# Hybrid convolution and attention, eight images on one core: the next image's convolution, normalisation and the token mean put in other places

## The chip, the cores and the metric

One core of a Trainium2 chip runs the whole program. The metric is the device time of one execution in microseconds; a time is given as the median of runs. The profile is of one execution on the same core.

The engines by their names in the profile: PE is the matrix engine (PEld its weight loads), DVE the vector engine, ACT the engine for activation functions, POOL the general engine, and SP the engine whose queue issues nearly all DMAs here. All arithmetic is in fp32. PE works off one fp32 matmul as two instructions, so the counts of PE instructions in the profile are twice the counts in the program; transposes are one instruction.

## The reference, cut to what matters

There are 8 images of 32 x 32 positions with 256 channels, `S = 1024` positions ("tokens") each.

```python
# first layer: group norm (32 groups of 8 channels), then convolution beside attention
g = _gn(x)
conv_out = conv3x3(g, conv_w) + conv_b                 # 256 -> 192 channels
k, q, v = split(g @ qkv_w + qkv_b)                     # 8 heads of 8
logits = q @ k.T + rel_w(q) + rel_h(q)                 # relative logits by column and by row
attn = softmax(logits) @ v @ attn_w + attn_b           # 64 channels
x = x + concat([conv_out, attn])
# second layer: tokens
t = x.reshape(8, 1024, 256)
n = layernorm(t)
t = t + softmax(n @ W_q @ (n @ W_k).T / sqrt(128)) @ (n @ W_v) @ W_o + b_o + n
n2 = layernorm(t)
r = softmax(mean(n2, axis=tokens) @ Wr + br)           # one routing per image, two of 8 experts
t = t + layernorm_affine(experts(n2, r) + n2)
```

The mean of `n2` over the tokens of an image is needed only for the routing, after all eight images have passed the attention of the second layer.

## The kernel before, in words

**Phases.** A first phase runs over the images one after the other and does the first layer and the attention of the second; the finished tokens go to DRAM (`Td`). A second phase loads them again and runs the router and the experts. The change is in the first phase.

**Order.** PE's instructions run in the order in which the program is written (`manual_schedule` for PE). The other engines' instructions are ordered by the framework's scheduler, each engine's queue then running strictly in its order. Work is put between other work by generators: a function yields after a few instructions, and another one calls `next` where it wants them.

**One image, in the order of PE:**

1. `conv_layer_attention` (L559). Eight heads are handled in two groups of four and two halves of the queries, which makes four `Unit`s. A unit loads an operand `F` by 24 DMAs on SP: eight pairs of `rh` and `kq` (L436, L440), which the scores read, and eight `rwd` (L447), which the weights read too. In 8 steps a unit computes 16 score tiles (`score`, L464, tile `lg`, two buffers); DVE takes a maximum of each (L472), and after four heads two small operations (L476, L479). `fold` (L481) turns the maxima into a row of `F`: DVE writes `mb` (L490) and three DMAs on SP bring it in (L494). Then `weigh` computes the scores again, with everything added (L504, tile `st`), ACT takes the exponential (L512), and `gather` multiplies by the values (L520, tile `po`). Maxima run `lead` = 10 steps ahead of exponentials. In those ten steps there is nothing to weigh, and the convolution is put there: `conv_steps` (L403) does 8 tiles of 18 matmuls (L411), DVE adds each finished tile to the image (L419). Two tiles are computed ahead of the first score and eleven matmuls go into each step.
2. The last steps have no scores left, only weights and values. There `norm_steps` (L232) of the next image is put: transposes (`tpx`, L243), copies and statistics on DVE (L245, L246), two small matmuls (`pm`, `pv`), a square root on ACT, then the normalised image into `gpad` (L270), shifted copies of it (L284, L285) and copies by tiles `xn` (L278) on Pool, and the bias added to the image on Pool (L250).
3. The projection of the heads (`pp`, L623).
4. `attention_layer` (L627): layer norm, transposes (`tpn`, L647), keys, queries (`pq`, L662), values, scores (`lg1`), softmax, products (`po1`, L730) and projection (`pa1`, L742). Its `fill(us)` calls put in `input_steps` (L289) of the next image: keys and queries (`pk`, L296), values (`pvv`, L329), the relative logits by column (L364, "w") and by row (L367, "h", tile `prel`), and transposes of the first (`tpw`, L396).
5. The token mean: once the deviations of the second layer norm are known (`rs2`, L772 to L774), 16 matmuls of one column each (L781), two instructions each, and one for the correction (L788), into `pmt`; then `Td` is stored.

The loop over images begins with the load of the next image into `T`, which has two buffers, so that the load reuses the buffer of the image before:

```python
for b in range(B):
    T[b + 1] = load_image(b + 1) if b + 1 < B else None
    ...
    conv_layer_attention(b, ..., norm_steps(b + 1, nxt) ...)
    ...
    attention_layer(b, fill)
    fill(1000.0)
```

The tile pools of PSUM are `lg` (2 buffers of two banks), `st` (3) and `po` (1).

Of the kernel before, what the change touches and what calls it, by code (L numbers as in the profile page):

```python
# [16 lines left out]
P = 128  # L17
# [18 lines left out]
def kernel(  # L36
# [54 lines left out]
    with ExitStack() as ph:  # L91
# [17 lines left out]
        def lg_tile(name):  # L109
            return ps_lg.tile([P, 2, 512], FP, tag="lg", name=name)  # L110

# [120 lines left out]
        def norm_steps(b, held):  # L232


            both = f_tile("x").rearrange("p a e s -> p a (e s)")
            xT = both[:, 0].rearrange("p (k s) -> p k s", k=KC)
            st = work.tile([P, KC, 2, 6], FP, tag="gst", name="gst", bufs=2)
            mv = work.tile([P, KC, 2], FP, tag="gmv", name="gmv", bufs=2)
            for kc in range(KC):
                for q in range(2):  # L240
                    tp = st_tile("tpx").rearrange("p (j t) -> p j t", j=4)
                    for j in range(4):
                        nc.tensor.transpose(tp[:, j, :], T[b][:, q * 4 + j, kc * P : (kc + 1) * P], ident)  # L243
                    dst = xT[:, kc, q * 512 : (q + 1) * 512]
                    nc.vector.tensor_copy(dst, tp.rearrange("p j t -> p (j t)"))  # L245
                    nc.vector.bn_stats(st[:, kc, q, :], dst)  # L246
                    yield
                nc.vector.bn_aggr(mv[:, kc, :], st[:, kc].rearrange("p q s -> p (q s)"))
# [12 lines left out]
            yield  # L261
# [5 lines left out]
            nc.vector.reciprocal(gr, gr)  # L267
            for kc in range(KC):
                xv = xT[:, kc, :].rearrange("p (h w) -> p h w", w=WW)
                nc.vector.tensor_scalar(  # L270
                    gpad[:, 1, kc, 1 : HH + 1, :], xv, gm[:, kc, :], gr[:, kc : kc + 1], ALU.subtract, ALU.mult
                )

            xn = both[:, 1].rearrange("p (k j t) -> p k j t", k=KC, j=NT)
# [7 lines left out]
            for kc in range(KC):  # L282
                mid = gpad[:, 1, kc, 1 : HH + 1]
                nc.gpsimd.tensor_copy(gpad[:, 0, kc, 1 : HH + 1, 1:WW], mid[:, :, 0 : WW - 1])  # L284
                nc.gpsimd.tensor_copy(gpad[:, 2, kc, 1 : HH + 1, 0 : WW - 1], mid[:, :, 1:WW])  # L285
            held["xn"] = xn
            yield

        def input_steps(b, held):  # L289


            kq = work.tile([P, S], FP, tag="kq", name="kq")
            for q in range(2):
                pk = st_tile("pk")
                for kc in range(KC):
# [7 lines left out]
                    yield 0.86  # L303
# [23 lines left out]
            for j in range(NT):  # L327
# [8 lines left out]
                yield 0.43  # L336
# [17 lines left out]
            for which in range(2):  # L354
                for half in range(2):
                    prs = lg_tile("prel")
                    for i in range(16):
# [16 lines left out]
                        if i % 4 == 3 and i < 15:  # L374
                            yield 0.7
# [13 lines left out]
                    yield 0.7  # L389

            for t2 in range(NT // 2):
# [9 lines left out]
                yield 0.43  # L401

        def conv_steps(b):  # L403

            n = 9 * KC
            for t in range(NT):
                pc = st_tile("pc")
# [14 lines left out]
        class Unit:  # L422
# [91 lines left out]
            def gather(self, j, parts):  # L514

                if self.po is None:
                    self.po = ps_po.tile([P, 512], FP, tag="po", name="po")
# [41 lines left out]
        def conv_layer_attention(b, kq, rh, rwd, rwq, ahead):  # L559
# [5 lines left out]
            conv = conv_steps(b)  # L565
            left = NT * 9 * KC - 2 * 9 * KC
            lead = NT + LAG
            for _ in range(2 * 9 * KC):
                next(conv)
            for s in range(NU * NT + lead + 2):  # L570
# [21 lines left out]
                else:  # L592
                    if weigh:
                        units[w].weigh(k, (1, 3), lg_tile)
                        units[w].weigh(k, (0,), st_tile)
                        units[w].weigh(k, (2,), st_tile)
                    if gather:
# [3 lines left out]
                if not weigh and left:  # L601
                    todo = -(-left // (lead - s))
                    for _ in range(todo):
                        next(conv)
                    left -= todo
                if s % NT == 0 and 0 < u <= NU:
                    units[u - 1].fold(u - 1)
                if s > NU * NT:
                    next(ahead, None)
            for _ in ahead:  # L610
                pass
# [13 lines left out]


        def attention_layer(b, fill):  # L627


# [23 lines left out]
            fill(5.6)  # L653

# [71 lines left out]
            def gather(ib):  # L726
                po = ps_po.tile([P, 512], FP, tag="po", name="po1")
# [49 lines left out]
            fill(2.0)  # L777
            pmt = st_tile("pmt")
            for kc in range(KC):
                for t in range(NT):  # L780
                    nc.tensor.matmul(  # L781
                        pmt[:, kc : kc + 1],
                        lhsT=T[b][:, t, kc * P : (kc + 1) * P],
                        rhs=m[:, t, 1:2],
                        start=t == 0,
                        stop=t == NT - 1,
                    )
# [4 lines left out]
            nc.sync.dma_start(out=Td[b], in_=T[b])  # L792

        with tc.manual_schedule(engines={mybir.EngineType.PE}):
            held = {}
            for _ in norm_steps(0, held):
                pass
            for _ in input_steps(0, held):
                pass
            for b in range(B):  # L800
                T[b + 1] = load_image(b + 1) if b + 1 < B else None
                nxt = {}
                conv_layer_attention(
                    b,
                    *(held[k] for k in ("kq", "rh", "rwd", "rwq")),
                    norm_steps(b + 1, nxt) if b + 1 < B else iter(()),
                )
                steps = input_steps(b + 1, nxt) if b + 1 < B else iter(())

                def fill(us):  # L810
                    while us > 0:
                        took = next(steps, None)
                        if took is None:
                            break
                        us -= took

                attention_layer(b, fill)
                fill(1000.0)
                held = nxt
                del T[b]  # L820

# [266 lines left out]
```

## Time and profile before

| | us |
|---|---|
| time, median of 3 runs (lowest to highest) | 2812.09 (2807.95 to 2813.89) |
| the profiled execution's own time | 2810.18 |
| its span, first to last instruction | 2808.4 |
| PE busy | 2676.2 |
| DVE busy | 1358.4 |
| ACT busy | 972.9 |
| Pool busy | 292.4 |
| granted PE clock, mean over the span (1 is full) | 0.935 |

One image in the profile, the fourth, by its stages (times from the start of the span; the other images lie within a few microseconds):

| stage | from | to | us | mean granted clock |
|---|---|---|---|---|
| end of the last projection (`pa1`) to the first exponential's matmul (L504) | 896.2 | 969.1 | 72.9 | 0.91 |
| scores and weights together | 969.1 | 1048.5 | 79.4 | 1.00 |
| end of the first layer, with the next image's norm | 1048.5 | 1087.3 | 38.8 | 1.00 |
| `pk` to `pq`: next image's inputs beside the layer norm | 1087.3 | 1121.8 | 34.5 | 0.63 |
| attention of the second layer | 1121.8 | 1175.5 | 53.7 | 0.98 |

A row of a timeline gives the start, the time, the engine, the line and the instructions. The granted clock is the share of PE's full clock that the chip's throttle let through. SP's rows are the issuing of DMAs, not the transfers.

### The profile page before, as it was taken

Reading aid. Unit: us, or ns where it says so; the run is one execution under the profiler, and the core shown is the slowest. Engines: PE = TensorE matmul, PEld = TensorE weight load, DVE = VectorE, ACT = ScalarE, POOL = GpSimd, SP = SyncE. Lnnn points to the kernel's source line nnn. Section 1 sums busy time; section 2 is a strip of 40 time slices with the busy share of each in tenths; the row PEclk is TensorE's granted clock in tenths of the full one; section 3 lists DMA queues with packets and bytes.
Section 4 is the critical chain, followed back from the end, with each engine's and each line's share of the span. In section 5 each row is a group of like instructions: output and inputs, shape, how many; then the busy total and the mean of one; then the engine's idle time right before and its main releaser. Section 6 shows DMA issues by size and latency. Waiting matters only on the chain.

```text
span 2808.4 us, 42236 instructions
## 1 busy us (share of the span) xinstructions
PE 2676.2 (95%) x17737; PEld 1643.9 (59%) x17737; DVE 1358.4 (48%) x2415; ACT 972.9 (35%) x1614; POOL 292.4 (10%) x319
## 2 busy tenths in 40 slices
PE   5999999999999999999999999999999879999998
PEld 4735673567357735773576367636763456666665
DVE  3574357335733573367336733673366343322332
ACT  0054305431543164316431542163226422222222
POOL 5003000300030003000300030003000121111110
PEclk7998899889988998999799989997999979999999
DMA  3510141014102410242023202320322031121110
GB/s 96 86 33 20 38 85 33 21 49 73 33 21 54 68 33 21 56 66 34 20 59 63 34 20 62 61 34 20 66 41 34 1 109 60 60 75 60 60 53 23
DMA packets 83757, 135.86 MB, mean 48 GB/s; under 512 B 12000, under 2 KB 40552, under 8 KB 81520
## 3 DMA queue, kind: packets, MB, share of 16 engines
q1 hardware_dynamic: 80976, 131.20, 21.0%
q8 instruction: 140, 2.29, 0.4%
q10 hardware_dynamic: 2592, 1.97, 0.2%
q14 instruction: 49, 0.40, 0.1%
HBM read 53.43 MB, written 25.17 MB: 28 GB/s over the span
## 4 chain that ended last, share of the span: by engine, by line
PE 90%; DVE 4%; ACT 3%; DMA 2%; issue 1%; POOL 0%; ACTq 0%; SPq 0%; DVEq 0%
PE pc L411 14%; PE lg L464 14%; PE po L520 9%; PE py L1019 8%; PE phd L1001 8%; PE st L504 8%; PE po L730 4%; PE prel L364 3%; PE lg L699 3%; PE pq L662 2%; PE prel L367 2%; PE tp L719 2%; PE pmt L781 2%; PE py L1016 1%; ACT PT L512 1%; PE tpn L647 1%
## 5 line engine op out<-in xcount | busy, mean ns | idle before, releaser
L512 ACT ACTIVATE PT<-st 128x512 f32<-128x512 f32 (+1 forms) x944 | 541.6, 633 | 863.0 <-PE st L504 862.9
L472 DVE TENSOR_REDUCE my<-lg 128x32 f32<-128x1024 f32 x512 | 616.8, 1223 | 256.9 <-PE st L504 129.6
L504 PE MATMUL st<-F,km 32*128 32x512 f32 x2048 | 573.0, 646 | 14.1 <-ACT PT L512 8.1
L464 PE MATMUL lg<-km,F 24*128 24x512 f32 x2048 | 484.0, 636 | 0.0
L411 PEld LDWEIGHTS pc<-convw,gpad 128*128 128x128 f32 x2304 | 387.3, 196 | 60.7 <-issue 59.9
L411 PE MATMUL pc<-convw,gpad 128*128 128x192 f32 x2304 | 412.6, 338 | 0.0
L520 PE MATMUL po<-PT,v 128*32 128x256 f32 (+1 forms) x3200 | 310.6, 456 | 2.9 <-ACT PT L512 2.7
L520 PEld LDWEIGHTS po<-PT,v 128*32 128x32 f32 x3200 | 64.2, 108 | 315.2 <-issue 282.4
L504 PEld LDWEIGHTS st<-F,km 32*128 32x128 f32 x2048 | 194.2, 185 | 85.5 <-ACT PT L512 44.4
L1019 PE MATMUL py<-w,hT 128*128 128x256 f32 x1024 | 237.3, 385 | 0.0
L464 PEld LDWEIGHTS lg<-km,F 24*128 24x128 f32 x2048 | 135.9, 183 | 152.1 <-issue 107.0
L1001 PE MATMUL phd<-n2T,w 128*128 128x512 f32 x512 | 224.2, 596 | 0.0
L1019 PEld LDWEIGHTS py<-w,hT 128*128 128x128 f32 x1024 | 190.1, 190 | 45.4 <-issue 22.4
L250 POOL TENSOR_TENSOR T<-T,l0b 128x2048 f32<-128x2048 f32 x8 | 36.2, 4524 | 1562.3 <-PE tpx L243 1562.3
L1026 DVE TENSOR_TENSOR r<-py,n 128x256 f32<-128x256 f32 x64 | 27.2, 425 | 310.8 <-PE py L1019 310.8
L1001 PEld LDWEIGHTS phd<-n2T,w 128*128 128x128 f32 x512 | 97.3, 192 | 115.2 <-issue 108.0
L730 PE MATMUL po<-pt,qkv 128*128 128x256 f32 x512 | 116.6, 381 | 11.3 <-DVE pt L722 11.3
L1008 ACT ACTIVATE hT<-phd,b1c 128x512 f32<-128x512 f32 x128 | 86.3, 686 | 96.9 <-PE phd L1001 96.7
L699 PE MATMUL lg<-qkv 128*128 128x512 f32 x256 | 119.1, 593 | 0.0
L730 PEld LDWEIGHTS po<-pt,qkv 128*128 128x128 f32 x512 | 96.7, 190 | 36.2 <-DVE pt L722 13.2
L708 DVE TENSOR_REDUCE nm<-lg 128x1 f32<-128x1024 f32 x64 | 78.0, 1219 | 72.5 <-PE lg L699 72.5
L364 PEld LDWEIGHTS prel<-kq,bdw 32*128 32x128 f32 x1024 | 101.5, 291 | 15.5 <-issue 15.0
(213 smaller groups left out, 2482.7 us busy)
## 6 DMA issues: line engine op xcount, KB each, us to landing
F<-rh SPq DMA_DIRECT2D x256, 128.0 KB
F<-kq SPq DMA_DIRECT2D x256, 64.0 KB
F<-rwd SPq DMA_DIRECT2D x256, 64.0 KB
w<-in_L_ffn_W_dram SPq DMA_DIRECT2D x32, 512.0 KB
T<-in_x_dram SPq DMA_DIRECT2D x8, 1024.0 KB
rwd<-rw SPq DMA_DIRECT2D x16, 512.0 KB
Td<-T SPq DMA_DIRECT2D x8, 1024.0 KB
T<-Td SPq DMA_DIRECT2D x8, 1024.0 KB
```

Of the source, the lines that this page charges most:

```text
L364: nc.tensor.matmul(dst, lhsT=lhsT, rhs=kqv[rows, :, a], start=True, stop=True)
L411: nc.tensor.matmul(pc[:, 0:CO], lhsT=gflat[:, dx, kc, t * P + dy * WW : (t + 1) * P + dy * WW], rhs=convw[:, i, :], start=i == 0, stop=i = ...
L464: nc.tensor.matmul(lg[:, a, :], lhsT=self.F[r : r + 24, a, 0, i * P : (i + 1) * P], rhs=KM[self.g][r : r + 24, a].rearrange("p e k -> p (e ...
L472: nc.vector.tensor_reduce(my[:, :, hl], lg.rearrange("p a (y x) -> p y a x", y=WW), AX.XY, ALU.max)
L504: nc.tensor.matmul(st[:, i, :] if len(heads) > 1 else st, lhsT=KM[self.g][r : r + 32, a, e, :], rhs=self.F[r : r + 32, a, e, :], start=Tru ...
L512: nc.scalar.activation(self.pts[j][:, hs, :], st, AF.Exp)
L520: nc.tensor.matmul(self.po[32 * hl : 32 * hl + 32, cols], lhsT=v32[:, j, self.g * HG + hl, :], rhs=self.pts[j][:, hl, cols], start=j == 0, ...
L699: nc.tensor.matmul(lg[:, h, :], lhsT=qk[0][:, i * P : (i + 1) * P], rhs=qk[1][:, h * 512 : (h + 1) * 512], start=True, stop=True,)
L730: nc.tensor.matmul(po[:, 0:IB], lhsT=v1[:, jc, :], rhs=pt[:, jc, :], start=jc == 0, stop=jc == NT - 1)
L1001: nc.tensor.matmul(phd, lhsT=ws[k][0][:, kc, f * P : (f + 1) * P], rhs=n2T[:, kc, q * 512 : (q + 1) * 512], start=kc == 0, stop=kc == KC - 1,)
L1008: nc.scalar.activation(hT[:, k * NF + f, :], phd, AF.Gelu, bias=b1c[:, f, k * B + b : k * B + b + 1])
L1019: nc.tensor.matmul(py, lhsT=hT[:, k * NF + f, j * P : (j + 1) * P], rhs=ws[k][1][:, f, :], start=False, stop=k == TOPK - 1 and f == NF - 1,)
```

## The change

It moves four things.

- **Norm of the next image.** `norm_steps(b + 1)` now runs in the ten steps of the first maxima of image `b` instead of in the last steps: one piece after each step from the third on. The part that writes `gpad` waits until the convolution of image `b` is done. Its transposed image lies in a `pt` buffer, and the copies by tiles are a function of their own, called after the first layer.
- **Convolution.** A class `Conv` holds an image's convolution. After each sixteenth of the relative logits of the next image, four matmuls of that image's convolution follow, 64 in all, into the one `po` tile; `whole()` completes the tile that is begun (72 of 144). The rest runs in the next call of `conv_layer_attention`: 30 matmuls ahead of the first score instead of 36, what is left over the ten steps. The first image has no such work ahead of it and keeps its whole convolution there.
- **Token mean.** Pool multiplies the eight tiles of the finished image by the deviations and adds them up (DVE does it for the last image). `token_mean` then needs three matmuls, which come in the third step of the next image's maxima.
- **Order of the weights in the last steps.** The heads 0 and 2 come ahead of the pair 1 and 3.

```diff
+        def po_tile(name):
+            return ps_po.tile([P, 512], FP, tag="po", name=name)
...
-        def norm_steps(b, held):
-            both = f_tile("x").rearrange("p a e s -> p a (e s)")
-            xT = both[:, 0].rearrange("p (k s) -> p k s", k=KC)
+        def norm_steps(b):
+            xT = pt_tile("xT").rearrange("p (k s) -> p k s", k=KC)
...
             nc.vector.reciprocal(gr, gr)
+            yield None
             for kc in range(KC):
...
+        def by_tiles():
+            xn = f_tile("x").rearrange("p a e s -> p (a e s)")[:, 0 : KC * S]
...
         def input_steps(b, held):
...
                         if i % 4 == 3 and i < 15:
-                            yield 0.7
+                            yield 0.7, True
...
-        def conv_steps(b):
+        def conv_steps(b, place):
             for t in range(NT):
-                pc = st_tile("pc")
+                pc = place[0]("pc")
...
-            conv = conv_steps(b)
-            left = NT * 9 * KC - 2 * 9 * KC
-            for _ in range(2 * 9 * KC):
-                next(conv)
+            left = conv.left
+            go = True
+            first = min(left, 30)
+            conv.run(first)
+            left -= first
...
                     if weigh:
-                        units[w].weigh(k, (1, 3), lg_tile)
                         units[w].weigh(k, (0,), st_tile)
                         units[w].weigh(k, (2,), st_tile)
+                        units[w].weigh(k, (1, 3), lg_tile)
...
-                if not weigh and left:
+                if not weigh:
                     todo = -(-left // (lead - s))
-                    for _ in range(todo):
-                        next(conv)
+                    conv.run(todo)
                     left -= todo
+                    if s > 1 and go:
+                        go = next(between, None)
+                elif s == lead:
+                    for _ in between:
+                        pass
...
-                if s > NU * NT:
-                    next(ahead, None)
...
             fill(5.6)
+            whole()
...
-            fill(2.0)
-            pmt = st_tile("pmt")
-            for kc in range(KC):
-                for t in range(NT):
-                    nc.tensor.matmul(pmt[:, kc : kc + 1], lhsT=T[b][:, t, ...], rhs=m[:, t, 1:2], ...)
+            acc = work.tile([P, C], FP, tag="n", name="acc", bufs=2)
+            if b + 1 < B:
+                part = work.tile([P, C], FP, tag="n", name="part", bufs=2)
+                for t in range(NT):
+                    to = part if t else acc
+                    nc.gpsimd.tensor_scalar(to, T[b][:, t, :], m[:, t, 1:2], None, ALU.mult)
+                    if t:
+                        nc.gpsimd.tensor_tensor(acc, acc, part, ALU.add)
+            else:
...
+            nc.sync.dma_start(out=Td[b], in_=T[b])
+            return acc, mr
+        def token_mean(b, acc, mr):
+            for kc in range(KC):
+                nc.tensor.matmul(pmt[:, kc : kc + 1], lhsT=acc[:, kc * P : (kc + 1) * P], rhs=ones[:, 0:1], ...)
+            nc.tensor.matmul(pmt[:, KC : KC + NT], lhsT=ones, rhs=mr, start=True, stop=True)
...
+            conv = Conv(0)
             for b in range(B):
...
+                conv.place[0] = st_tile
+                conv_layer_attention(b, ..., conv, between())
+                held, conv = {}, Conv(b + 1)
...
                 def fill(us):
                     while us > 0:
-                        took = next(steps, None)
+                        took, small = next(steps, (None, None))
                         if took is None:
                             break
                         us -= took
+                        if small:
+                            conv.run(4)
```

## The prediction

> **What bounds the kernel now.** I read the page's busy times first, then the timeline of one image, the tensor engine's granted clock by stage, and SP's queue. All times are of the fourth image, the others agree.
>
> ```profile
> PE 2676.2 (95%) x17737; PEld 1643.9 (59%) x17737; DVE 1358.4 (48%) x2415; ACT 972.9 (35%) x1614; POOL 292.4 (10%) x319
> PEclk7998899889988998999799989997999979999999
> ```
>
> PE is busy 95% of the span, so only work that leaves PE, PE's idle places or its clock can pay. The clock row dips once or twice an image. The stretches show where (columns: length, busy us of PE, PEld, DVE, ACT, POOL, granted clock, DMA):
>
> ```profile
> 1091.00:1094.50 3.50, 3.50 (x35) 3.43 (x33) 2.38 (x11) 2.47 (x4) 0.00 (x0) 1.00 0.03 6
> 1106.00:1113.00 7.00, 7.00 (x54) 5.86 (x52) 1.11 (x3) 0.06 (x1) 4.86 (x3) 0.50 0.00 0
> 1113.00:1120.00 7.00, 7.00 (x257) 6.92 (x256) 1.30 (x2) 2.53 (x4) 1.11 (x1) 0.50 0.39 154
> 1178.10:1185.30 7.20, 7.17 (x35) 7.20 (x36) 0.09 (x1) 0.95 (x1) 0.00 (x0) 0.52 0.30 100
> 1185.30:1189.00 3.70, 3.70 (x13) 3.70 (x14) 0.39 (x2) 0.00 (x0) 0.00 (x0) 0.55 0.78 229
> ```
>
> In the relative logits (rows two and three) PE is busy throughout but at half clock: they stream only 32 columns per instruction. The value matmuls before them (64 columns) keep 1.00. The token mean (row four, one column each) is cold too, and the first convolution after it starts cold. The chain of waits over the image's end:
>
> ```profile
> 1174.37 1.15 PE pa L742 x4
> ...
> 1177.78 0.21 DVE mv L774
> 1177.99 0.14 issue
> 1178.13 6.72 PE pmt L781 x32
> 1184.85 0.43 PE pmt L788 x2
> 1185.29 13.51 PE pc L411 x72
> 1198.80 1.07 PE lg L464 x8
> ```
>
> PE waits 2.6 us for the deviations, spends 7.2 us on the mean, then convolves. Last, SP's queue in the next lead (start, time, what):
>
> ```profile
> 905.77 0.39 SPq L104 DMA_DIRECT2D T<-in_x_dram  x1
> 906.21 0.62 SPq L436 DMA_DIRECT2D F<-rh  x1
> ...
> 948.10 4.84 SPq L447 DMA_DIRECT2D F<-rwd  x8
> 965.44 30.90 SPq L494 DMA_DIRECT2D F<-mb  x6
> ```
>
> From the image load to the last of the F loads SP issues for 47.2 us (44.8 to 52.0 over six images, middle 47.3), and only then the F<-mb that the first exponentials need. Now there are 12.5 us to spare.
>
> Let zero be the end of an image's last projection matmul (1175.5 in the chain, 896.2 in the SP rows). The first exponential's matmul (L504) starts at +71.5 in five of the six following leads, +72.9 in one.
>
> **Term 1, convolution between the relative logits (seven images): +17.4 us each.** Now the stretch from pk (L296) to pq (L662) takes 33.4 to 34.9, mean 34.2. The change adds 72 convolution matmuls (144 instructions): sixteen blocks of four, and eight at the end. An instruction takes 162.5 ns at full clock, the first of a block 100 ns more. A block: 1.4 us and 0.2 for switching in and out. Does the clock stay up? From the records I computed, per 3.41 us (the step in which the granted clock changes), the array's use: columns streamed times the share of rows and columns used, over what the full clock could do. The clock fell after use of 0.34 or less, held from about 0.4, and rose from 0.5 only after 0.39 or more. A mixed step is about 0.55 (four convolutions, 3072 column-passes, in 2.2 to 2.9 us): it holds if entered warm, and pk and pvv before it are warm. Cold it would be 0.32 and stay cold, a rival below. Warm: pk and pvv 7.3; eight w steps of 0.92 (pairs every 112 ns, as at 1094.5) plus 1.6: 20.2; eight pairs of LN transposes at 0.34: 2.7; eight h steps of 0.55 (half of 6.98/8, plus 0.1) plus 1.6: 17.2; two waits for the single po tile inside a block, 0.6 each (0.35 for L419 and the handover): 1.2; transposes of rw 1.1; last eight convolutions 2.7. That is 52.4. pq then starts warm: 6.9 instead of about 7.7. Sum +18.2 - 0.8 = +17.4, bounds 15 to 20; times seven, +122. The trace has no h step at full clock; at today's rate the term is 3 us an image higher, inside the bounds.
>
> A page speaks here. The Trainium skill (TensorE: Matmul & The Clock Gate, Part 1) has the clock full after one busy window of about 3.4 us. By busy time that fails: 7.00 busy of 7.00 at clock 0.50. If the page's rule held literally, the logits would gain nothing from company and the total would be some 46 us worse.
>
> **Term 2, norm out of the end of layer one (seven images): -5.1 us each.** From the last lg to the end of pp it takes 38.5 to 40.8 (mean 39.4); in the eighth image, which has no next norm, 34.3. The difference holds four transpose groups, two small matmuls and the Sqrt/Exp table loads. The new order of the heads may give ACT another 0.1 us a step; ACT rests 0.26 to 0.58 there. Sum -36, bounds -30 to -45.
>
> **Term 3, end of image to the first exponential (images two to seven).** Removed: the 2.6 wait, 7.2 of mean, about 1.5 of cold convolution, and half the convolution. What is late next?
> - PE: 30 convolutions 10.0, then ten steps of 1.1 (lg) and 1.6 (four convolutions and a switch), norm 3.3: ends at 40.
> - DVE: from +10.6, eighteen maxima of 1.23 before mb, 22.1; four L476/L479 pairs 2.7; evacuations 0.7; norm copies and statistics 5.5; the small norm steps 2.9 (L258 took 1.6); mcol and mb 1.0; mean 0.4; gaps 1. Ends near +47. The four tpx steps make it DVE's lead, not PE's.
> - SP: the load of the next image reuses the buffer of the finished one and so now waits for Pool's sum instead of PE's mean. In the changed program's order for SP that wait stands, as now, ahead of F's last rh and kq for the first unit, its eight rwd, all of the next two units, and F<-mb. Pool starts at +2.6 and the load needs fifteen operations less the last add: eight multiplies and six adds, 128x256. Nearest rows: L648, 740 ns for such an add; L966, 2852 ns for a 1024-column multiply, 0.75 us for 256 by its slope. I take 0.75 and 0.05 between: 11.2, so the load issues at +13.8 (bounds 0.57, the slope of L250, to 0.9: +11 to +16). Now it issues at +9.6 or so. Then 47.3 of issues, and 2.2 for F<-mb to land (between 2.0 at 1054.5 and 3.3 at 2167.0): +63.3.
>
> The fourth maximum needs the last rh and kq, which landed 8.3 us after the load issue (914.0 against 905.8): PE stands from about +13 to +22, DVE with it, so DVE's end moves to +55. SP's +63.3 still comes last. PE is then idle some 5 us just ahead of the main stage, and may enter it cold: there the use at half clock is near 0.39, so it can last some windows. I take 3 us, bounds 0 to 10. Gain 71.6 - 63.3 - 3 = 5.3; times six, -32.
>
> The other page is on Pool: the Trainium skill (GPSIMD Engine Reference, Engine selection) calls two-input elementwise work about twice as slow there as on VectorE. Rows: 740 ns against 425 for L1026 of that size. Doubling 425 as an estimate, the load would issue at +15.2 and the total be 8 us worse.
>
> **Term 4, image eight:** no load follows and SP is not held. Its F loads ended at +47.7, so +49.9, and 3 for a cold start: -18.6. **Term 5, image one:** the whole convolution stays in its lead, which is PE's: the next norm's transposes add +3. **Term 6, the last mean:** eight DVE operations of 0.48 and three matmuls take the place of 16 cold ones: 0. Td's store keeps its place; Pool's bias and copies for the norm end long before pvv reads them.
>
> Sum: 122 - 36 - 32 - 19 + 3 = +38 us on the profiled execution's own 2810.2 (span 2808.4): 2848. The median of the runs is 1.9 above that: **2850**.
>
> **Rivals.** *The queue keeps up (faster).* Place: SP's stretch between load and F<-mb. Part of its 0.78 us per issue is waiting for landings (the waits put about 17 us an image on F's own loads). If those waits shrink, or Pool's sum is short, DVE's +49 (+47 and landing) sets the lead: -22.5 an image, image eight -31, no restart: 122 - 36 - 135 - 31 + 3 = -77, 2735. It decides as soon as the first exponential comes before about +57 with the clock kept warm 3 us of restart included. Half way is 2790. For it: so much of the wait is landing; against it: the issues alone cost 0.60 and 0.68. *The clock stays half in the mixed stretch.* Each convolution block doubles (+1.3), w steps and transposes stay as now: about +31 an image, 3065. For it: cold use 0.32 is self-keeping; against it: warm entry. Dips at single images would add 31 each. *No change:* the gains just cover term 1, which needs 6 us more per lead.
>
> **How the numbers follow.** About 0.2% (5.6 us) is what a measurement can tell from no change. Main case, slower through terms 1 and 3: 0.66, its own range 2795 to 2925 (term 1 at 15 or 20, load at +11 or +16, restart 0 to 10). Clock half: 0.07. Faster: 0.22. Same: 0.05. The range reaches down to 2765, into the faster case, and leaves out its far end and the cold case.
>
> **What would show it.** The granted clock near 1.00 through the prel lines, and pk to pq near 52; T<-in_x_dram about 14 us after the last pa, waiting for POOL; lg of the second step waiting for DMA F<-kq or F<-rh; L504's first start at about +63 right after F<-mb. Wrong if pk to pq is 45 or less, if L504 starts before +57, or if PEclk falls to 0.5 there.

## The result and the profile after

The changed kernel takes 2935.4 us (median of four runs, 2922.0 to 2937.5) against 2812.5: slower by a factor of 1.043 (95% interval 1.040 to 1.046). The forecast was 2850 with a range of 2765 to 2925: the right sign, and the loss three times as large as forecast. The profiled execution took 2921.98 (span 2919.9), the shortest of its runs, and 111.5 more than the one before by their spans. What follows accounts for these 111.5; the 13 us by which the median lies above the profiled execution are in no trace.

First the page's busy row and clock row. The work on PE is 20 us less, the span 111 us longer: PE now waits. The clock row dips about as often as before, but in other places.

```profile
PE 2655.7 (91%) x17513; PEld 1571.1 (54%) x17513; DVE 1341.5 (46%) x2423; ACT 979.2 (34%) x1616; POOL 381.9 (13%) x424
PEclk8999989997999798989998999889989879999999
```

Next, stretches of the changed kernel (length, busy us of PE, PEld, DVE, ACT, POOL, granted clock, DMA): the relative logits by column and by row with the convolution between them, and then the start of a main stage (from the first exponential's matmul to the last score).

```profile
844.30:862.60 18.30, 17.85 (x173) 16.11 (x172) 3.89 (x8) 1.94 (x3) 6.43 (x7) 0.98 0.04 9
864.50:880.30 15.80, 15.35 (x309) 13.19 (x311) 1.41 (x3) 2.07 (x4) 0.55 (x1) 1.00 0.17 68
1000.70:1007.00 6.30, 0.00 (x0) 0.00 (x0) 0.00 (x0) 0.00 (x0) 1.65 (x2) 0.61 0.44 55
1007.00:1020.00 13.00, 12.86 (x44) 5.43 (x44) 4.35 (x5) 4.56 (x8) 0.00 (x0) 0.50 0.01 1
1020.00:1027.00 7.00, 7.00 (x60) 2.03 (x56) 4.10 (x4) 3.64 (x7) 0.00 (x0) 0.82 0.00 0
```

The logits hold the clock now (0.98 and 1.00 where it was 0.50), but for one step of 3.4 us at half clock around their start, which five of the seven images have. In row three no engine but Pool does anything: PE waits for a DMA. Row four is the price: 13 us at half clock with PE busy all the time.

The lead of that image, by the chain of waits (start, us, what). The image before ended at 938.1.

```profile
952.61 0.93 POOL part L792
953.56 0.39 SPq L104
953.99 0.62 SPq L443
954.66 7.15 DMA F<-kq
961.94 2.04 PE lg L471 x2
...
994.38 0.58 DVE mb L497
...
1000.71 6.39 DMA F<-mb
1007.14 2.10 PE st L511 x6
```

The load of the next image (L104) waits for Pool's last sum; the last kq of the first unit stands behind it, and PE waits for that. DVE has written `mb` at 995.0, but F<-mb goes out only at 1000.7. SP's rows say what it did in between:

```profile
994.26 0.68 SPq L447 DMA_DIRECT2D F<-kq  x1
994.98 4.92 SPq L454 DMA_DIRECT2D F<-rwd  x8
1000.71 2.52 SPq L501 DMA_DIRECT2D F<-mb  x3
```

Last, ACT at the end of the first layer (image eight, all images have it), and PE at the same time:

```profile
2291.24 1.28 ACT L540 ACT_TABLE_LOAD   x1
2292.53 0.20 ACT L540 ACTIVATE tab<-PT 128x1 f32<-128x1 f32 x1
2292.75 1.28 ACT L519 ACT_TABLE_LOAD   x1
2294.04 1.02 ACT L519 ACTIVATE PT<-st 128x1024 f32<-128x1024 f32 x1
2296.55 0.58 ACT L544 COPY os<-po 128x512 f32<-128x512 f32 x1 [1.48 <-PE po L527]
2297.15 1.28 ACT L88 ACT_TABLE_LOAD   x1
```

```profile
2295.12 1.38 PE L527 MATMUL po<-PT,v 128*32 128x512 f32 x6 [3.23 <-ACT PT L519]
...
2300.00 3.67 PE L631 MATMUL pp<-aw,aT 64*128 64x64 f32 x16
```

`tab` (L540) is a one-column square root that brings in its table early; it reads head 2. In the old order head 2 came last. In the new order it is finished before the pair 1 and 3, so ACT loads the table of the square root, then that of the exponential again for the last pair, then the other once more. PE waits 3.2 us for the last pair, and `pp` runs cold (3.67 us, 2.00 where it is warm). The same place in the kernel before, where the load stands behind the last exponential:

```profile
2188.93 2.00 ACT L512 ACTIVATE PT<-st 128x1024 f32<-128x1024 f32 x3 [0.26 <-PE st L504]
2190.95 1.28 ACT L533 ACT_TABLE_LOAD   x1
2192.24 0.20 ACT L533 ACTIVATE tab<-PT 128x1 f32<-128x1 f32 x1
```

The change by stages, in us summed over the images, from the two traces (another 1 us lies between them):

| stage | predicted | measured |
|---|---|---|
| `pk` to `pq`, and the first layer norm's attention behind it | +122 | +121 |
| last score to end of `pp`, eight images | -36 | -8 |
| lead of images two to seven | -50 | -30 |
| main stage of images two to seven | +18 | +35 |
| image eight, lead and main stage | -19 | -13 |
| image one | +3 | 0 |
| after the last projection | 0 | +5 |

### The profile page after: what moved, and what is told of

It reads as the page before. It is cut to its first block, busy times and chain, and to the rows that moved or that the text cites. A ratio compares the mean times of both kernels' runs of the same rounds, so it can differ in the third digit from the quotient of the medians.

```text
span 2919.9 us, 41895 instructions
## 1 busy us (share of the span) xinstructions
PE 2655.7 (91%) x17513; PEld 1571.1 (54%) x17513; DVE 1341.5 (46%) x2423; ACT 979.2 (34%) x1616; POOL 381.9 (13%) x424
## 4 chain that ended last, share of the span: by engine, by line
PE 79%; DVE 8%; DMA 6%; ACT 3%; POOL 3%; issue 1%; SPq 1%; ACTq 0%; DVEq 0%
PE lg L471 13%; PE pc L418 10%; PE po L527 9%; PE py L1072 8%; PE phd L1054 8%; PE st L511 7%; PE po L740 4%; PE lg L709 3%; DVE my L479 3%; PE prel L371 2%; DMA F<-mb 2%; PE pq L672 2%; PE tp L729 2%; PE py L1069 1%; PE prel L374 1%; DMA F<-kq 1%
## 5 line engine op out<-in xcount | busy, mean ns | idle before, releaser
L471 PE MATMUL lg<-km,F 24*128 24x512 f32 x2048 | 567.1, 669 | 56.5 <-DMA F<-kq 55.7
L418 PE MATMUL pc<-convw,gpad 128*128 128x192 f32 x2304 | 447.7, 344 | 6.3 <-DVE T L426 6.3
L527 PE MATMUL po<-PT,v 128*32 128x256 f32 (+1 forms) x3200 | 324.3, 466 | 28.9 <-ACT PT L519 25.9
L471 PEld LDWEIGHTS lg<-km,F 24*128 24x128 f32 x2048 | 169.4, 194 | 246.4 <-issue 119.7
L511 PEld LDWEIGHTS st<-F,km 32*128 32x128 f32 x2048 | 182.7, 192 | 159.5 <-issue 61.5
L1079 DVE TENSOR_TENSOR r<-py,n 128x256 f32<-128x256 f32 x64 | 27.2, 424 | 310.9 <-PE py L1072 310.9
L657 POOL TENSOR_TENSOR T<-T,n 128x256 f32<-128x256 f32 x64 | 47.0, 740 | 705.1 <-DVE n L652 705.1
L553 DVE RECIPROCAL rc<-pa 128x16 f32<-128x16 f32 x32 | 8.2, 257 | 231.1 <-PE pa L550 231.1
```

What stands on the lines that cost most here:

```text
L418: nc.tensor.matmul(pc[:, 0:CO], lhsT=gflat[:, dx, kc, t * P + dy * WW : (t + 1) * P + dy * WW], rhs=convw[:, i, :], start=i == 0, stop=i = ...
L471: nc.tensor.matmul(lg[:, a, :], lhsT=self.F[r : r + 24, a, 0, i * P : (i + 1) * P], rhs=KM[self.g][r : r + 24, a].rearrange("p e k -> p (e ...
L511: nc.tensor.matmul(st[:, i, :] if len(heads) > 1 else st, lhsT=KM[self.g][r : r + 32, a, e, :], rhs=self.F[r : r + 32, a, e, :], start=Tru ...
L527: nc.tensor.matmul(self.po[32 * hl : 32 * hl + 32, cols], lhsT=v32[:, j, self.g * HG + hl, :], rhs=self.pts[j][:, hl, cols], start=j == 0, ...
```

## The experiments

Means by stage of all runs, from their traces (lead: end of the last projection to the first exponential's matmul, images two to seven; main: from there to the last score, images two to eight; tail: to the end of `pp`, eight images). Ends are taken at the start of the last instruction, so a lead is 0.4 us longer here than counted from the prediction's zero. The ratio is to the kernel before, timed on the same chip.

| kernel | lead | main | tail | `pk` to `pq` | median us | ratio (95%) |
|---|---|---|---|---|---|---|
| before | 72.1 | 79.4 | 38.8 | 34.3 | 2812.5 | 1 |
| after | 67.2 | 85.2 | 37.7 | 52.6 | 2935.4 | 1.043 (1.040 to 1.046) |
| e1_order | 67.2 | 84.8 | 34.6 | 50.8 | 2884.1 | 1.025 (1.024 to 1.027) |
| e2_mb_act | 60.3 | 81.2 | 38.4 | 53.0 | 2851.2 | 1.013 (1.010 to 1.015) |
| e3_noconv | 74.9 | 79.3 | 38.2 | 36.8 | 2837.5 | 1.009 (1.007 to 1.011) |
| e4_dvesum | 58.7 | 85.1 | 38.1 | 52.6 | 2882.2 | 1.026 (1.022 to 1.029) |
| e5_order_mb | 61.2 | 81.2 | 34.7 | 51.1 | 2816.1 | 1.002 (1.001 to 1.004) |
| e6_three | 52.5 | 81.2 | 34.9 | 51.1 | 2768.0 | 0.984 (0.982 to 0.985) |
| e7_three_noconv | 64.8 | 81.4 | 34.4 | 35.7 | 2748.6 | 0.977 (0.975 to 0.980) |
| e8_warm | 69.0 | 81.4 | 38.3 | 52.6 | 2916.0 | 1.036 (1.033 to 1.039) |
| e9_load_late | 70.4 | 80.0 | 37.7 | 52.4 | 2913.1 | 1.037 (1.035 to 1.039) |
| e10_mb0_noconv | 64.9 | 106.4 | 34.5 | 34.5 | 2945.1 | 1.047 (1.046 to 1.049) |
| e11_mb0_w | 56.4 | 106.4 | 34.4 | 39.8 | 2915.4 | 1.039 (1.036 to 1.042) |
| e12_mb0_two | 56.9 | 106.7 | 34.5 | 50.7 | 2994.8 | 1.062 (1.057 to 1.067) |
| e13_three_w | 55.3 | 82.0 | 34.4 | 40.3 | 2719.5 | 0.967 (0.966 to 0.968) |

My theory was that four separate costs add up: the convolution between the logits, SP's queue in the lead, the cold start that this brings, and the order of the heads. The rivals were that the lead is DVE's anyway, that the transfers and not the queue are late, and that the mixing alone is to blame.

**The order of the heads alone.**

```diff
-                        units[w].weigh(k, (0,), st_tile)
-                        units[w].weigh(k, (2,), st_tile)
                         units[w].weigh(k, (1, 3), lg_tile)
+                        units[w].weigh(k, (0,), st_tile)
+                        units[w].weigh(k, (2,), st_tile)
```

> The changed kernel with one thing put back: the steps of the tail weigh heads (1,3) before 0 and 2, as before. Theory (the table): the Sqrt table pre-load reads head 2, which in the new order is done before the pair (1,3), so ACT loads Sqrt, loads Exp again for the last pair and loads Sqrt once more; PE waits 3.2 us and projects cold. Then the stretch from the last lg to the end of pp falls from 36.5 to 39.0 to about 34.3 in all eight images, 3.5 us each, and the total falls by about 28 us, to some 2907. Rival (the order of the heads has nothing to do with it; the tail is held by gathers and transposes): the stretch stays at 37 to 39 and the total within 5 us of 2935.

The tail is 34.6 in the mean (34.4 in most images), what the prediction had. `pk` to `pq` behind it gains 1.8 as well. The span is 38 us shorter than the changed kernel's, 25 of it in the tail. The median falls by 51 where I had forecast 28: `pk` to `pq` accounts for 13 more, and the rest is the changed kernel's profiled execution being the shortest of its runs. ACT's rows at the end of image eight have one table load, after the last exponential:

```profile
2257.18 2.00 ACT L519 ACTIVATE PT<-st 128x1024 f32<-128x1024 f32 x3 [0.26 <-PE st L511]
2259.20 1.28 ACT L540 ACT_TABLE_LOAD   x1
2260.49 0.20 ACT L540 ACTIVATE tab<-PT 128x1 f32<-128x1 f32 x1
```

**F<-mb on another queue.**

```diff
-                    nc.sync.dma_start(out=F[r, a], in_=mb[c]...)
+                    nc.scalar.dma_start(out=F[r, a], in_=mb[c]...)
```

> The changed kernel with the six F<-mb loads of each fold issued on ACT's queue instead of SP's. Theory (SP's queue ends the lead): DVE has mb at about +57 after the last projection, and the loads now go out then instead of at +58 to +63; with 2 to 6 us to land the first exponential's matmul comes at +60 to +63 instead of +66 to +69, 25 to 35 us off the total, some 2905; the cold start of the main stage stays. Rival A (the transfers themselves are behind the F<-rwd transfers, whichever queue issues them): first matmul within 1.5 us of +66.8, total within 8 us. Rival B (DVE's maxima end the lead): the same as the theory in time of issue, but no gain at all.

The lead is 60.3, at the lower edge of what the theory said; rivals A and B fall. ACT issues within 0.1 us of DVE's `mb`, and the first matmul follows 3.2 us after the issue instead of 6.4:

```profile
989.08 1.76 ACTq L501 DMA_DIRECT2D F<-mb  x3
992.28 1.40 PE L511 MATMUL st<-F,km 32*128 32x512 f32 x6 [0.51 <-DMA F<-mb]
```

The gain is 84 us, far more than forecast, because with a wait of 0.5 us in place of 4.4 to 9.5 the main stage starts warm too: 81.2 instead of 85.2. I had expected the cold start to stay.

**No convolution between the logits.** The lines `if small: conv.run(4)` are taken out.

> The changed kernel with no convolution between the relative logits: all 144 convolution matmuls of an image stand in its lead, the rest of the change stays. Theory (the moved half costs its full time there, and in the lead it fills time in which PE waits for SP's queue): pk to pq falls from 52.4 to 34 (-18.5 for seven images, -129); the lead takes 23 us more of PE work into about 27 us of idle places, so the first exponential comes at +67 to +71; PE enters the main stage with little idle time before it, so the cold start shrinks by 0 to 5 us an image. Total 2935 - 129 + 15 - 20 = about 2800 (2775 to 2830). Rival (what slows the kernel is the lead itself: the norm and Pool's sum): the lead grows by the whole 23 us of the convolution and the total stays at 2935 - 129 + 160, no faster than before the experiment.

`pk` to `pq` falls by 15.8 and not 18.5, the lead grows by 7.7, the main stage is warm. The rival, a lead longer by 23, falls. At 2837.5 the total misses the range by 7 us; the lead is above what I gave it, since the wait for the last kq stays (the waits have "PE lg L471 <- DMA F<-kq" at 46.9 us in 6 times, against 55.7 in the changed kernel), and the convolution cannot fill it, as it stands behind it on PE.

**The sum on DVE for all images.**

```diff
-            if b + 1 < B:
+            if False:
```

> The changed kernel with the token sum on DVE for all images (eight operations of 0.48 us, as in the last image), none of it on Pool. Theory (the image load waits for Pool's sum and all later issues of SP wait behind it): the load issues at about +7.5 instead of +15.5, SP's chain ends 8 us earlier, and DVE's maxima, 3.5 us later by the sum but no longer stalled as long, end the lead: first exponential at +59 to +63 instead of +66.8, 25 to 45 us off the total, some 2900. Rival (what ends the lead is not SP, but DVE): DVE has 3.5 us more to do and the total rises by up to 20 us.

The load goes out at about +8, and SP's wait for it is 15.5 us in all instead of 61.8:

```profile
SPq L104 <- DVE acc L798: 15.5, 6, 2.7
```

The lead is 58.7, slightly better than forecast, and the total 53 us lower where 25 to 45 were forecast. F<-mb still goes out only when SP is through with the F loads and lands about 6 us later, and the main stage is as cold as before. So the load's wait for Pool is worth 8.5 us an image and the queue another cost of its own.

**Repairs together.** The next three have the old order and F<-mb on ACT (e5), the sum on DVE too (e6), and no mixing besides (e7).

> The changed kernel with the old order of the heads in the tail and F<-mb on ACT's queue, both together; the token sum stays on Pool. Theory (the two costs are separate): lead 60.4 as with ACT's queue alone, main stage 81.2, last lg to end of pp 34.4 and pk to pq 50.6 as with the old order alone; with 52.3 for the first layer's attention and 0.2 that is 279.1 an image against 279 before, a total of about 2800 (2790 to 2815). Rival (ACT is late with the loads once its order is changed back, or the gains overlap): 2835 or more.

> As the kernel before in this list, and the token sum on DVE too, so that the image load does not wait for Pool: all three repairs. Theory (with SP out of the way DVE's maxima end the lead, and the fourth maximum no longer stands for the last kq): first exponential at +50 to +56, main stage 79.4 to 81.2, tail 34.4, pk to pq 50.6, first layer 52.3; 267 to 275 an image, a total of 2715 to 2770, faster than the kernel before the change. Rival (DVE, with 3.9 us of sums more, already ends the lead at +60): no faster than with Pool's sum, about 2800 to 2825.

> All three repairs and no convolution between the relative logits. Theory (72 convolution matmuls cost 16 us there and 23 us where PE sets the time; with the repairs the lead is PE's as soon as it holds the whole convolution): pk to pq 34 to 37, lead 66 to 74, main stage 79.4, tail 34.4, first layer 53.5: 268 to 279 an image, a total 0 to 50 us above that of the three repairs alone. Rival (the mixed stretch is dear and the lead would hold all of it for nothing): the total is 20 us or more below that of the three repairs alone.

The costs add up as stages: e5 is about level with the kernel before, a microsecond above its range, and e6 is faster by 1.6%, at the upper end of its range. In e6 the last 20 us of the lead's chain are DVE's, SP is out of it, and PE goes warm into the main stage:

```profile
949.79 2.27 DVE my L479 x2
...
952.56 0.59 DVE mb L497
953.18 3.16 DMA F<-mb
956.38 1.40 PE st L511 x6
```

That the mixing alone is to blame falls with e6, which keeps all of it and is faster than the kernel before; still, taking it out alone (e3) gave the largest gain of a single change, 98 us. For e7 the theory had the sign wrong and the rival was right to within a microsecond: 19 us faster without the mixing than with it, where I had expected 0 to 50 slower and the rival 20 or more the other way. The mixed half costs 15.4 us between the logits (51.1 against 35.7) and saves 12.3 in the lead, because the lead goes from PE's 64.8 to DVE's 52.5 and no further.

**The cold start alone.** 24 matmuls of the convolution's shape stand ahead of the first exponential's matmul (their sums are used by nothing).

> The changed kernel with 24 more matmuls of the convolution's shape (7.8 us at full clock), whose sums nothing uses, just ahead of the first exponential's matmul of images two to eight, where PE waits 9.5 us for F<-mb. Theory (the idle time ahead of the main stage lets the clock fall, and at half clock the stage's own use of the array does not bring it back for four to six windows): the main stage takes 79.4 to 80.5 instead of 84.4 to 86.8, the lead at most 1 us more; some 35 us off the total, about 2900. Rival (the main stage is longer because DVE or ACT still work off the lead's maxima): it stays at 84 to 87, the total at 2935 or above.

In images two to five the main stage is 79.2 to 79.3, and in the stretch of the fourth the clock stays at 1.00 where the changed kernel had 0.50. In images six to eight it is 83.7 to 84.7: there a wait of 0.9, 2.2 and 4.3 us was left behind the added matmuls. The lead is 1.8 longer, and the total misses the forecast of about 2900 by 16 us. So idle time ahead of the stage, and not work left over on DVE or ACT, is what makes it 5 to 7 us longer. How long the idle time must be is open: 0.9 us was enough in image six, 0.5 us was not in e2, and I did not vary it.

**The load behind the first two units on SP.**

```diff
             units = [Unit(n, kq, rh, rwd) for n in range(2)]
+            if b + 1 < B:
+                T[b + 1] = load_image(b + 1)
...
-                if not last:
-                    T[b + 1] = load_image(b + 1)
```

> The changed kernel with one thing moved: the next image's load stands on SP's queue behind the F loads of the first two units instead of ahead of the first unit's last one. Pool still sums, F<-mb is still on SP. Theory (what costs is that SP stands at the load until Pool is done, not the number of its issues): the first unit's last kq goes out some 13 us earlier, the fourth maximum no longer stands for it, and the first exponential comes at +54 to +61 instead of +66.8; 35 to 75 us off the total, 2860 to 2900. Rival (SP's own issues fill the lead, whatever they wait for): first exponential at +64 or later, total within 15 us of 2935. A second way to miss: the load now lands at about +30, so the transposes of the next image wait for it and hold the maxima behind them on PE.

The theory's number missed, by the way of missing that was named last: the load goes out at +29 to +31, and the transposes of the next norm, which stand in PE's order ahead of the maxima, wait for it.

```profile
964.79 1.57 PE L418 MATMUL pc<-convw,gpad 128*128 128x192 f32 x8
985.80 1.11 PE L245 MATMUL tpx<-ident,T 128*128 128x128 f32 x4 [19.44 <-DMA T<-in_x_dram]
```

The lead grows to 70.4, but the stage behind it starts warm (79.2 to 79.3 in six of seven images), since now DVE is late and not SP: PE waits 0.5 us for F<-mb. The total falls by 22 us, a second sight of the cold start alone. It does not tell the wait at the load from the number of issues; e4 does.

It does settle what made F<-mb slow to land. The loads are on SP's queue here too. In images two to seven the last rwd loads lie 12 us ahead of them, and the first matmul follows 3.2 us after the issue, as from ACT's queue in e2; in image eight they stand right behind rwd loads, and it takes 6.4. The fourth image:

```profile
992.16 4.05 SPq L454 DMA_DIRECT2D F<-rwd  x8
1008.25 1.82 SPq L501 DMA_DIRECT2D F<-mb  x3
```

So rival A of e2 has a part in the cost: some 3 us of the lead are the loads just ahead, the rest is the wait for SP. Whether another queue avoids the 3 us when rwd loads are under way no run shows; in e2 none was issued in the 14 us before.

**F<-mb of the first unit alone on ACT.** `nc.scalar` for n = 0, `nc.sync` for the others, with the other repairs; three amounts of mixing.

> All three repairs and no convolution between the relative logits, but F<-mb on ACT's queue for the first unit of an image alone; the other three units' stay on SP, where nothing waits for them. Theory (the main stage took 81.2 instead of 79.4 because ACT waits for mb and issues nine loads between its exponentials): main stage back to 79.4, lead 64 to 65, total about 2734 (2725 to 2742). Rival (the 1.8 us come from the table load of Exp or from the clock at the start of the stage): main stage 81, total 2748 as with all folds on ACT.

> As the one before in this list, with four convolution matmuls after each step of the relative logits for the width (36 of 144, with the four that complete a block), none after those for the height. Theory (DVE ends the lead at +52, PE at +64 with the whole convolution, so half of what was mixed is free in the lead, and the width's steps, which were cold alone, run at full clock in company): lead 52 to 56, pk to pq 41 to 46 with the height's steps cold again; main stage 79.4; 260 to 268 an image, a total of 2690 to 2720. Rival (a convolution matmul between logits costs its full 0.33 us and more): pk to pq 48 or more, total no better than without mixing.

> As the one before in this list, with two convolution matmuls after every step of the relative logits (36 in all) instead of four after half of them. Theory (the array's use decides the clock): two convolutions with 0.92 or 0.55 us of logits are a use of about 0.40 to 0.45 at full clock, just over what held it so far; if it holds, pk to pq is 39 to 42 and the total 2670 to 2700. Rival (the use of the mixed step lies under what holds the clock): the stretch runs at 0.5, each pair of convolutions takes 1.3 us instead of 0.65, pk to pq 45 to 50, total 2720 to 2750.

All three are failures as wholes, by a cause I had not looked for: their main stages take 106 us. The scheduler's order for SP's queue changed with what is on it. With all F<-mb on SP those of the second unit stood ahead of the fourth unit's loads; here they stand behind them, and these wait for an F buffer. SP in e10, where the exponentials of the second unit wait 23.7 us (the last row joins the loads of two folds):

```profile
441.36 5.72 SPq L454 DMA_DIRECT2D F<-rwd  x8
456.36 0.61 SPq L443 DMA_DIRECT2D F<-rh  x1
...
467.41 5.84 SPq L454 DMA_DIRECT2D F<-rwd  x8
474.00 39.62 SPq L501 DMA_DIRECT2D F<-mb  x6
```

The question of e10, why the main stage is 81.2 and not 79.4 with all folds on ACT, has no experiment that isolates it. Its rival (the table load of Exp, or the clock at the start of the stage) falls by e9, whose ACT loads that table there too, and whose main stage starts warm in six images and takes 79.2 to 79.3 with F<-mb on SP. That leaves the issues on ACT, which the trace of e7 shows: ACT issues F<-mb in the midst of the exponentials and rests 2.85 us around it, and the waits of that stage have a second rest of 2.8.

```profile
429.57 1.87 ACTq L501 DMA_DIRECT2D F<-mb  x3
431.49 1.08 ACT L519 ACTIVATE PT<-st 128x512 f32<-128x512 f32 x2 [2.85 <-DMA F<-mb]
```

The stages ahead of the main one still tell about the mixing. With half of it among the column logits (e11) `pk` to `pq` is 39.8, only 5.3 above none. With two matmuls after every step (e12) there are two sorts of image: 37.5 in two of them, below the theory's 39 to 42, and 48 to 61 in the other five, most of them above the rival's 45 to 50. The same stretches of e12, column logits and row logits of a slow and of a fast image:

```profile
281.30:308.90 27.60, 27.60 (x169) 24.23 (x170) 4.83 (x10) 1.94 (x3) 9.71 (x9) 0.52 0.05 9
311.30:330.20 18.90, 18.90 (x285) 15.39 (x284) 1.05 (x2) 1.66 (x4) 0.00 (x0) 0.50 0.14 56
592.10:607.50 15.40, 15.40 (x171) 13.75 (x170) 5.05 (x10) 1.96 (x3) 7.33 (x9) 1.00 0.09 18
608.70:619.30 10.60, 10.60 (x285) 8.71 (x284) 1.21 (x3) 2.56 (x4) 1.89 (x1) 1.00 0.26 102
```

The work is the same and PE is busy for the whole of both; only the clock differs. By the array's use, worked out from the records as in the prediction, the slow image has about 0.2 to 0.33 in the windows of the cold stretch and the fast one about 0.4 to 0.56: two states that each keep themselves. The Trainium skill (TensorE: Matmul & The Clock Gate, Part 1) gives the clock back after one busy window of about 3.4 us. Here it stays away for the 46.5 us of rows one and two, all of it busy time (as are the 2.4 us between them), so busy time alone does not bring it back; the use fits both images.

**Half of the mixing, all folds on ACT.** Four convolution matmuls after each step of the column logits, none after the row logits, and all repairs.

```diff
                         if i % 4 == 3 and i < 15:
-                            yield 0.7, True
+                            yield 0.7, which == 0
...
-                    yield 0.7, True
+                    yield 0.7, which == 0
```

> All three repairs, F<-mb of all units on ACT's queue, and four convolution matmuls after each step of the relative logits for the width only (36 of 144). Theory (mixing costs less than it saves only as long as the lead is PE's): by the stages of the run with the same half mixed but split queues, pk to pq 40 against 35 without mixing and 51 with all of it, lead 56 against 64 and 53; main stage 81.2; tail 34.4; first layer 52.4: 264.2 an image against 269 without mixing and 273 with all, a total of 2710 to 2730, against 2748.6 and 2768. Rival (mixing never pays, a convolution matmul between logits costs what it costs in the lead): 2745 to 2760, between the two.

2719.5 us: 0.967 of the kernel before (0.966 to 0.968), within the forecast range and the best of all. The clock row has no dip from the second slice to the routing (a slice is 68 us; within it the row logits still fall to half clock, for 3 to 7 us an image):

```profile
PE 2563.4 (95%) x17513; PEld 1539.6 (57%) x17513; DVE 1374.9 (51%) x2479; ACT 955.8 (35%) x1600; POOL 294.9 (11%) x319
PEclk8999999999999999999999999999999979999999
```

The rival (mixing never pays) falls: the first 36 matmuls cost 4.6 us between the logits (40.3 against 35.7), as they keep the column logits at full clock, and save 9.5 in the lead (55.3 against 64.8). The second 36 cost another 10.8 and save only 2.8.

## Why the prediction was right and wrong

**Right.** The direction, and the wait that ends the lead. Term 1 was 52.4 for `pk` to `pq`, measured 52.6; with what follows +122 against +121. The clock held in the mixed stretch, as the use of 0.55 said. The stall of the fourth maximum for kq came where forecast, +14.4 to +24 (forecast +13 to +22). SP's queue ended the lead, not DVE: `mb` was ready at +57 (forecast +55) and issued at +58 to +63. The faster rival had the right bound but needed more than it named: with the load out at +8 (e4) SP still issues F<-mb up to 5 us behind `mb`. Only with F<-mb off SP as well does the first exponential come at +52, before the +57 that the rival named; with the old order of the heads too, the kernel is then faster (e6).

**Term 2 failed by a wrong step**, the largest single error: -36 forecast (bounds -30 to -45), -8 measured, 28 of the 73 us missing from the sum. The prediction took the new order of heads for a matter of 0.1 us a step and looked at ACT's rests. What it left out is that `tab` reads head 2 of the last tile, so that the new order puts the table load ahead of the last exponential. In image eight, whose last steps held no norm before either, one load of 1.28 us became three. The trace of before showed the load right behind the last exponential, and the diff showed what moves; following the one reader of `pt[:, 2]` would have found it. e1 confirms it: 34.6 with the old order.

**Term 3 was right in mechanism and wrong in three sizes**, the restart among them (below); together they miss by 37 us, from -32 to +5. The first exponential came at +66.8 in the mean, not +63.3. Pool's pair of operations took 1.83 us a tile (0.92 and 0.72 and gaps), not 1.6: the load went out at +15.5 instead of +13.8. SP's chain behind it was a little shorter than the 47.3 taken. But F<-mb took 5.0 to 6.9 us from issue to use, not 2.2. Eight rwd transfers had been issued just before it; from the same queue, 12 us behind them, it took 3.2 (e9). The two sizes make 20 us over six images. The Trainium skill (GPSIMD Engine Reference, Engine selection) calls two-input elementwise work about twice as slow on Pool as on VectorE and one-input work "roughly line-rate". The adds agree with it roughly (0.72 on Pool; 0.42 for an add of that size on DVE, L1079). The multiplies by one value per partition, with a single tile as input, are the slower ones on Pool: 0.92 there, 0.35 for the same on DVE in the last image. It is they that made the load late (0.92 where 0.75 was taken; the adds took less than that).

**The restart after the idle time was mis-sized**: 3 us taken, 5 to 7.4 measured (the main stage is 84.4 to 86.8 instead of 79.4), +35 instead of +18. The bounds of 0 to 10 held it. The prediction saw that the stage's use at half clock is near the point at which the clock comes back and still took the low end; the clock stayed at half for 12 to 18 us of the stage. e8 and e9 show that idle time is the cause, e2 that a lead without it starts warm.

**Term 6**: the first transposes of the experts' phase come 5.6 us later. The mean itself is ready as early as before (PE's last `pmt` ends 8.2 us after the last projection, 8.4 before the change). The delay is behind it, in DVE's queue between routing and normalisation; I did not test why.

Two of these errors, the table loads (28 us) and the landing (some 24), were absent from the range's bounds, and the median passed the range by 10 us. The profiled execution itself, 2922.0, lay 3 us inside it.

## What to carry to other kernels

Before reordering independent work, look for whoever reads one of its pieces as a signal: a table preload, a buffer's release, a wait on "the last one". When work leaves PE, the next bound is often a queue that issues in strict order; put the one transfer that everybody waits for on a queue of its own, and check with the new order of the old queue what else moved. And fill a stretch that runs at half clock with just enough dense work to keep the clock up: here 36 matmuls cost 4.6 us where 72 cost 15.4.

## What the runs showed that was not expected

- The granted clock held one of two states under the same instructions: 37.5 or 60.7 us for one stretch with PE busy throughout (e12). By the working above it fell after windows with a use of 0.35 to 0.38 and held from about there, so little decides which one holds.
- Idle time of 4 to 11 us ahead of a dense stage cost 5 to 7 us more behind it, at half clock.
- The three F<-mb loads were there 3.2 us after their issue from ACT's queue (e2) and from SP's where no load had just gone ahead of them (e9), and 5 to 7 us after it right behind eight rwd loads (the changed kernel, e4).
- Moving three DMAs of one unit to another queue changed the scheduled order of the rest on SP and cost some 25 us per image (e10 to e12).
